# One transformer block on one core: sums of exponentials deferred by the work left, first V products ahead of the rows, last outputs in the scores' PSUM banks

## The chip, the core and the metric

One core of a Trainium2 chip runs the whole program. The metric is the device time of one execution in microseconds (us); the profiler's trace of one such execution gives the times of single instructions. PE is TensorE, DVE is VectorE, ACT is ScalarE, POOL is GpSimd, SP is SyncE, which issues most DMAs here.

## What is computed

Eight sequences (B=8) of N=1024 rows, D=512; context of 1024 rows with 384 columns. Everything is float32. Cut to what matters:

```python
def block(x, ctx, ...):                      # x (8,1024,512)
    # kind 1: cross attention, 8 heads of 64
    y = layernorm(x); q = y @ Wq; k, v = ctx @ Wk, ctx @ Wv
    a = softmax(q k^T / 8); x = x + tanh(g1) * ((a v) @ Wo + bo)
    # kind 2: self attention, 16 heads of 32, with gates over heads
    y = layernorm(x); q, k, v = y @ Wq2 + bq, y @ Wk2 + bk, y @ Wv2 + bv
    q = (q / |q| + query_embedding) * softplus(temperature)
    h = softmax(q k^T / sqrt(32)) v
    gate = top-3 softmax gates of h @ Wr, with the shared gates of h @ Ws   # one number a row
    return x + tanh(g2) * ((h * gate) @ Wp + bp)
```

## The kernel before, in words

**Tiles and stages.** Work on attention goes by chunks of 128 columns of q and k: four chunks of kind 1 (two heads each) and four of kind 2 (four heads each) in each of the eight sequences; below, `one[c]` and `two[c]` are the chunks of a sequence, and a batch is a sequence. A chunk handles the queries in two halves h of 512. A step (`score`, L436, and `value`, L528) takes 128 x 2 x 512 scores twice into two PSUM tiles "sc", ACT makes exponentials "e" of them (two tiles of 128x1024), and PE multiplies e with V into "av". Kind 1 has 8 steps a chunk, kind 2 has 16 (8 in each half).

**Row maxima.** Scores are shifted by their maxima, which have to be known before the chunk's first step. So while one chunk attends, the maxima of the next are taken: PE makes a bf16 copy of the scores ("pm", L373) and DVE reduces it (L414 in pairs of 128x512, L397 in fours). A chunk of kind 2 has 34 such items, kind 1 has 18 (`pairs`, L433; the last two are a small reduction and a transposition). The result goes through four small DMAs into a row "sh" that PE adds to the scores.

**Sums of exponentials.** The softmax needs the sum of e over keys. POOL adds two e tiles (`paired`, L463 to L465); each such pair tile then goes either into an accumulator by an addition on DVE (L473) or stays as a further accumulator (`add`, L469). At the end of a half, `summed` (L483) sums all accumulators over the partitions on PE with a matrix of ones (L491): per round of accumulators 8 matmul records in kind 2 and 4 in kind 1. Then ACT takes Ln and Exp(-x), and POOL multiplies the attended half "hT" by it (`divided`, L519, L526). At most five pair tiles may be live: `room` (L599) empties the queue of postponed work, and where that is not enough sums early into a tile "part".

**What sets the order.** All engines but SP run in an order written out by the program itself. A planner keeps clocks `at["PE"]`, `at["DVE"]`, `at["POOL"]` in ns, with a cost per piece (L220 to L236): 950 for a product of 128 rows (MM), 300 for a pair of maxima on PE and 1380 on DVE, 1750 for an addition on DVE, 1000 for a round of sums. `later` holds postponed work with the clock at which it is due. `attend` (L643) runs a chunk's steps and, between them, fills in products for other stages (`fillers`, up to `cost` ns) and pairs of maxima. It sets `ontime` (L674), which decides in `add` (L472) whether a pair tile may go to DVE:

```python
ontime[0] = not maxima or not maxima.mx or maxima.done >= 1.25 * share * maxima.pairs   # L674
if accs and (self.kind == 1 and self.b or ontime[0] and at["DVE"] <= at["PE"] + 1000):  # L472
```

**The start** (L933 to L959) loads weights, context and rows, makes k of `one[0]`, normalizes and transposes the eight row tiles with five of the eight V products (`v1`, L741) between them, then q; then `pace` (L909) makes the maxima of `one[0]` beside projections. **The end** is `finish` (L782): for each half the gates ("pg"), `weights` (small DVE operations), and `outputs` ("po", L841: product with wp into PSUM, then x = po * gate + x on DVE, L847, and the store, L848). For the last sequence it fills the second half of the last chunk and runs on after it. `ln1` (L709) normalizes and transposes the rows of the next sequence beside `two[2]`; `load_rows` (L695) issues their loads.

Of the kernel before, what the change touches and what calls it, by code (L numbers as in the profile page):

```python
# [10 lines left out]
F32 = mybir.dt.float32  # L11
# [5 lines left out]
P = 128  # L17
# [4 lines left out]
def tile_gated_block(  # L22
# [44 lines left out]
    H = 512  # L67
# [21 lines left out]
        nc.sync.dma_start(out=xt, in_=x[b, ts(t, P), :])  # L89
        return xt  # L90

    def load_ctx(b, parts=1):
        ct = big.tile([P, NDC, N], F32, tag="ctx", name=f"ctx_{b}")
        src = cT[b].rearrange("(c p) n -> p c n", p=P)
        for h in range(parts):
            nc.sync.dma_start(out=ct[:, :, ts(h, N // parts)], in_=src[:, :, ts(h, N // parts)])
        return ct


# [158 lines left out]
    class Chunk:  # L258


        def __init__(self, kind, b, c):
            self.kind, self.b, self.c = kind, b, c
            self.key = f"{kind}_{b}_{c}"
            self.width = HD1 if kind == 1 else HD2
            self.nh = P // self.width
            self.nk = 4 // self.nh
            self.ns = NT // self.nk
            self.mx, self.done, self.free, self.waiting = None, 0, 0.0, False
            self.SC = 2200 if kind == 1 else 1250
            self.steps = [(h, s) for h in range(NH) for s in range(self.ns)]  # L270

# [197 lines left out]
        def add(self, h, s, u, a, last):  # L469

            accs = self.acc.setdefault((h, u), [])
            if accs and (self.kind == 1 and self.b or ontime[0] and at["DVE"] <= at["PE"] + 1000):  # L472
                nc.vector.tensor_tensor(accs[-1], accs[-1], a, ALU.add)  # L473
                dve(1750)
                live[0] -= 1
                ready = at["DVE"] + 500
            else:
                accs.append(a)
                ready = at["PE"]
            if last and s + 1 == self.ns:  # L480
                later.append((ready, self.summed, h, True))

        def summed(self, h, end):  # L483

            ps = gen(f"sum_{self.key}_{h}")
            accs = [self.acc.pop((h, u)) for u in range(self.nh // 2)]
            for n in range(max(map(len, accs))):
                for u, acc in enumerate(accs):
                    for j in range(2):
                        if n < len(acc):  # L490
                            nc.tensor.matmul(  # L491
                                ps[ts(2 * u + j, self.width), :],
                                lhsT=ones[:, 0 : self.width],
                                rhs=acc[n][:, j, :],
                                start=(n == 0),
                                stop=(n == len(acc) - 1),
                            )
# [12 lines left out]
            r = work.tile([P, H], F32, tag="r", name=f"r_{self.key}_{h}", bufs=1)  # L510
            if part is not None:
                nc.vector.tensor_tensor(r, ps, part, ALU.add)
                dve(700)
                ps = r
            nc.scalar.activation(r, ps, AF.Ln)
            nc.scalar.activation(r, r, AF.Exp, scale=-1.0)  # L516
            self.divided(h, r)

        def divided(self, h, r=None):  # L519

            if h not in self.halves:
                self.halves[h] = r
                return
            self.finished.add(h)
            hT, r = self.st.hT[h][:, self.c, :], self.halves[h] if r is None else r
            nc.gpsimd.tensor_tensor(hT, hT, r, ALU.mult)  # L526

        def value(self, step):  # L528

# [5 lines left out]
            for kk in range(self.nk):  # L535
# [13 lines left out]
                    self.paired(h, s, 0, e[0], e[1], True)  # L549
                if kk + 1 < self.nk:  # L550
                    yield
            if self.kind == 2 and s % 2 == 0:
                room(2, self, h)
                for u in range(2):
                    self.paired(h, s + 1, u, e[u], self.e[h, s + 1][u], u == 1)
# [8 lines left out]
        def attention(self, after, first):  # L564

            if first:  # L570
                self.begun()
                yield "begun"
            for m, step in enumerate(self.steps):
                if m + 1 < len(self.steps):
                    self.score(self.steps[m + 1])
                    yield
                elif after:
                    yield "ready"
                    after.begun()
                    yield  # L580
                yield from self.value(step)

        def begun(self):
            self.e, self.acc, self.parts, self.halves, self.finished = {}, {}, {}, {}, set()
            self.score(self.steps[0])

# [1 line left out]
    later, soon = [], []  # L588
    live, ontime = [0], [True]

    def due(ns):
        while soon and soon[0][0] <= ns:
            _, emit, *args = soon.pop(0)
            emit(*args)
        while later and later[0][0] <= ns:
            _, emit, *args = later.pop(0)
            emit(*args)

    def room(n, ch, h):  # L599

        while live[0] > 5 - n:
            if later:
                _, emit, *args = later.pop(0)
                emit(*args)
            else:
                ch.summed(h, False)
        live[0] += n
# [35 lines left out]
    def attend(  # L643
# [20 lines left out]
        def pairs(slack):  # L664
# [2 lines left out]
                return pair(maxima, slack)  # L667
            return bool(ahead and ahead.done + 3 < ahead.pairs and pair(ahead, slack))

        was = at["PE"]  # L670
        for got in ch.attention(after, first):
            attended += at["PE"] - was
            share = max(0, attended / total - since) / (1 - since)
            ontime[0] = not maxima or not maxima.mx or maxima.done >= 1.25 * share * maxima.pairs  # L674
            due(at["PE"])
            if got == "begun":
                fill()
# [28 lines left out]
        rs = small.tile([P, NT, 1], F32, tag="rs1", name=f"rs1_{st.b}")  # L706
        inverse(rs, st.mv)

    def ln1(st):  # L709

        st.yT = big.tile([P, ND, N], F32, tag="yT", name=f"y1T_{st.b}")
        xts = [load_rows(st, t, "xn") for t in range(2)]
        scaled(xts[0], xts[0], st.mv[:, 0, :])
        for t in range(NT):
            if t + 1 < NT:
# [7 lines left out]

    def begin(b):
        st = State()
        st.b = b
# [55 lines left out]
    def finish(st, other=None):  # L782
# [21 lines left out]
        def weights(h):  # L804
# [33 lines left out]
            dve(2600)  # L838
            yield

        def outputs(h):  # L841
            rt = rts[h]
            for t in range(NQ):
                ps = gen(f"po2_{b}_{h}_{t}")
                yield from out_project(ps, hT, w, h * NQ + t)
                x1 = st.x[h * NQ + t]
                nc.vector.scalar_tensor_tensor(x1, ps, rt[:, t, :], x1, ALU.mult, ALU.add)  # L847
                nc.sync.dma_start(out=out[b, ts(h * NQ + t, P), :], in_=x1)  # L848
                dve(750)
                yield  # L850

        if other:
            yield from beside(other, gates(0), ND)
            yield from weights(0)
            yield from beside(outputs(0), gates(1), ND)
            yield from weights(1)
            yield from outputs(1)
            return
        for h in range(NH):
            yield from gates(h)  # L860
            yield from weights(h)
            yield from outputs(h)

    def between(st, nxt):

# [92 lines left out]
    pace(one[0], fill, one[1], (14 + 15 + 14) * MM)  # L958
    run(fill, 1e9)  # L959
    prev = None  # L960
    for b in range(B):
# [20 lines left out]
        fill = [v1(nxt)] if nxt else []  # L982
        attend(two[0], two[1], True, fill, 25 * MM, two[1], two[2])
        two[3].loads()
        attend(two[1], two[2], False, [two[3].project(st)], 19 * MM, two[2], two[3], rate=1.6)
        st.w = load_w(wp2, f"wp2_{b}")
        if nxt:
            one = nxt.chunks[1]
            one[0].loads()
            fill = [ln1(nxt), one[0].project(nxt)]  # L990
            attend(two[2], two[3], False, fill, 9 * 2100 + 16 * MM, two[3], one[0], least=2100)
            one[1].loads()
            attend(two[3], one[0], False, [one[1].project(nxt)], 15 * MM, one[0], one[1])
            prev, st = st, nxt
# [41 lines left out]
```

## Time and profile before

| what | value |
|---|---|
| time, median of 3 runs (lowest, highest) | 5030.72 us (5029.25, 5033.06) |
| the profiled execution's own time | 5029.73 us |
| its span, first to last instruction | 5028.0 us |
| PE busy | 4823.4 us, 96% |
| DVE, POOL, ACT busy | 2908.8, 2552.2, 2314.1 us |
| granted TensorE clock, mean | 0.996 |
| one sequence in the middle (start of `two[0]` to the next) | 621 us |
| first part, until the scores of `one[0]` | 93.4 us |
| last part, after the last product with V | 29.6 us |

How to read it: a group of the profile gives line, engine, operation, tiles and count, then busy time in us and the mean of one in ns, then the idle time of the engine just before them and what ended it. Busy is the union over time, so matmuls that lie side by side in the array count once. In a timeline, a row has start (us), duration (us), engine, line and count, and in brackets the idle time before it with what ended it. Windows by stage have the stretch, its length, and per engine the busy us with the count of instructions.

### The profile page before, as it was taken

To read this page: it belongs to the slowest core of one execution; us is meant where nothing else is said; L and a number is where in the kernel's file an instruction comes from. 1 tells how busy PE (TensorE), PEld (TensorE's weight loads), DVE (VectorE), ACT (ScalarE), POOL (GpSimd) and SP (SyncE) were. 2 spreads that over 40 slices of the span, in tenths; PEclk is the share of its full clock that TensorE was granted. 3 is DMA by queue.
4 is the path that set the end of the run, shared out by engine and by line. 5 is a ranking of instruction groups with operands and counts; after the bars stand their busy time and mean duration, and the time that the engine had idled before them with its cause. 6 is when DMAs were issued, how large, how long until landed. Compare 5 with 4: busy or idle time off the path is not lost.

```text
span 5028.0 us, 83971 instructions
## 1 busy us (share of the span) xinstructions
PE 4823.4 (96%) x35760; PEld 1435.5 (29%) x35760; DVE 2908.8 (58%) x4073; ACT 2314.1 (46%) x3037; POOL 2552.2 (51%) x1352
## 2 busy tenths in 40 slices
PE   8999999999999999999999999999999999999998
PEld 2222232222322223222232222322223322233222
DVE  4556555565555755557555575555755556554665
ACT  3435634356343563435534356343662436524354
POOL 1635646356463664636536365363653636636465
PEclk9999999999999999999999999999999999999999
DMA  2010011100101001010010100101001010010000
GB/s 79 26 32 15 24 42 35 33 17 23 49 26 36 13 23 49 26 36 13 23 52 23 36 13 23 64 11 36 15 23 64 9 36 20 11 51 9 18 1 18
DMA packets 126215, 145.18 MB, mean 29 GB/s; under 512 B 14480, under 2 KB 75920, under 8 KB 125840
## 3 DMA queue, kind: packets, MB, share of 16 engines
q1 hardware_dynamic: 125552, 139.81, 8.7%
q8 instruction: 280, 4.59, 0.4%
q14 instruction: 95, 0.78, 0.0%
q10 hardware_dynamic: 288, 0.00, 0.0%
HBM read 122.47 MB, written 16.78 MB: 28 GB/s over the span
## 4 chain that ended last, share of the span: by engine, by line
PE 81%; DVE 8%; ACT 7%; issue 2%; POOL 1%; DMA 0%; SPq 0%; ACTq 0%; POOLq 0%; DVEq 0%
PE sc L453 21%; PE av L539 17%; PE po L244 8%; PE pq L244 8%; PE pm L373 7%; PE pk L244 7%; PE pv L244 5%; ACT e L460 5%; DVE mx L397 4%; PE sum L491 4%; DVE mx L414 3%; PE pt L215 1%; PE pn L244 1%; POOL e L465 1%; DVE e L473 1%
## 5 line engine op out<-in xcount | busy, mean ns | idle before, releaser
L465 POOL TENSOR_TENSOR e<-e,e 128x1024 f32<-128x1024 f32 x768 | 1850.0, 2424 | 1246.8 <-PE av L539 746.1
L460 ACT ACTIVATE e<-sc 128x1024 f32<-128x1024 f32 x1536 | 1490.1, 1021 | 1275.1 <-PE sc L453 1209.0
L414 DVE TENSOR_REDUCE mx<-pm 128x1 f32<-128x512 f32 x2320 | 1488.7, 686 | 947.6 <-PE pm L373 933.1
L453 PE MATMUL sc<-q,k 32*128 32x512 f32 (+1 forms) x6144 | 1113.4, 606 | 0.0
L539 PE MATMUL av<-e,v 128*32 128x512 f32 (+1 forms) x6144 | 1076.0, 609 | 0.0
L473 DVE TENSOR_TENSOR e<-e,e 128x1024 f32<-128x1024 f32 x402 | 676.2, 1694 | 327.0 <-POOL e L465 326.2
L373 PE MATMUL pm<-kb,qb 32*128 32x512 bf16 (+1 forms) x3072 | 623.1, 382 | 46.2 <-DVE mx L397 26.4
L397 DVE TENSOR_REDUCE mx<-pm 128x2 f32<-128x1024 f32 x376 | 434.8, 1219 | 294.4 <-PE pm L373 294.4
L453 PE MATMUL sc<-sh,ones_b 1*128 1x512 bf16 x3072 | 413.3, 384 | 76.6 <-ACT e L460 67.7
L453 PEld LDWEIGHTS sc<-q,k 32*128 32x128 f32 (+1 forms) x6144 | 419.7, 186 | 191.3 <-issue 184.6
L373 PEld LDWEIGHTS <-qb 32*128 32x128 bf16 (+1 forms) x3072 | 147.6, 91 | 928.0 <-issue 918.4
L539 PEld LDWEIGHTS av<-e,v 128*32 128x32 f32 (+1 forms) x6144 | 193.2, 117 | 602.1 <-issue 571.2
L244 PE MATMUL pq<-y1T,wq 128*32 128x512 f32 (+1 forms) x1568 | 246.9, 595 | 5.3 <-ACT q L308 2.8
L244 PE MATMUL pk<-y2T,wk 128*32 128x512 f32 x2048 | 241.6, 594 | 7.5 <-ACT qq L315 7.5
L244 PE MATMUL pq<-y2T,wq 128*32 128x512 f32 x2048 | 244.9, 595 | 3.2 <-ACT rn L340 3.2
L244 PE MATMUL pv<-wv,y2T 128*32 128x512 f32 x2048 | 241.3, 597 | 0.0
L453 PEld LDWEIGHTS <-ones_b 1*128 1x128 bf16 x3072 | 103.3, 91 | 468.0 <-issue 453.2
L244 PE MATMUL po<-wp,h2T 128*64 128x512 f32 (+1 forms) x1152 | 232.3, 597 | 0.0
L244 PE MATMUL po<-wo,h1T 128*32 128x512 f32 x2048 | 229.9, 594 | 1.1 <-ACT y2T L216 0.9
L491 PE MATMUL sum<-e,ones 128*32 128x512 f32 (+1 forms) x1464 | 224.6, 595 | 3.6 <-DVE e L473 3.4
L526 POOL TENSOR_TENSOR h2T<-h2T,r 128x512 f32<-128x512 f32 x64 | 81.5, 1273 | 250.6 <-ACT r L516 212.8
L244 PE MATMUL pk<-ctx,wk 128*32 128x512 f32 (+1 forms) x1176 | 191.6, 604 | 17.7 <-DMA ctx<-in_ctx 9.0
(108 smaller groups left out, 2885.5 us busy)
## 6 DMA issues: line engine op xcount, KB each, us to landing
x<-in_x SPq DMA_DIRECT2D x64, 256.0 KB
out<-x SPq DMA_DIRECT2D x64, 256.0 KB
xs<-in_x SPq DMA_DIRECT2D x56, 256.0 KB
xn<-in_x SPq DMA_DIRECT2D x56, 256.0 KB
ctx<-in_ctx SPq DMA_DIRECT2D x7, 1536.0 KB
wq<-in_L_xattn_Wq SPq DMA_DIRECT2D x32, 256.0 KB
wo<-in_L_xattn_Wo SPq DMA_DIRECT2D x8, 1024.0 KB
wk<-in_L_ffn_Wk SPq DMA_DIRECT2D x32, 256.0 KB
```

Of the source, the lines that this page charges most:

```text
L215: nc.tensor.transpose(pt[:, c, :], xn[:, ts(c, P)], ident)
L244: nc.tensor.matmul(ps[ts(j, w), :], lhsT=lhsT[:, ts(j, w)], rhs=rhs, start=start, stop=stop)
L373: nc.tensor.matmul(ps, lhsT=self.qb[ts(i, width), ts(c, P)], rhs=self.kb[ts(i, width), ts(kh, H)], start=True, stop=True,)
L397: nc.vector.tensor_reduce(out, tiles[u], AX.X, ALU.max)
L414: nc.vector.tensor_reduce(mx[:, i * NT + c, kh : kh + 1], ps, AX.X, ALU.max)
L453: nc.tensor.matmul(pss[j // 2][:, j % 2, :], lhsT=lhsT, rhs=rhs, start=(m == 0), stop=(m == 1))
L460: nc.scalar.activation(e[u], pss[u], AF.Exp)
L465: nc.gpsimd.tensor_tensor(one, one, two, ALU.add)
L473: nc.vector.tensor_tensor(accs[-1], accs[-1], a, ALU.add)
L491: nc.tensor.matmul(ps[ts(2 * u + j, self.width), :], lhsT=ones[:, 0 : self.width], rhs=acc[n][:, j, :], start=(n == 0), stop=(n == len(acc ...
L526: nc.gpsimd.tensor_tensor(hT, hT, r, ALU.mult)
L539: nc.tensor.matmul(self.av[ts(i, width), :], lhsT=st.v[:, kc, ts(self.c * self.nh + i, width)], rhs=e[j // 2][:, j % 2, :], start=(kc == 0 ...
```

## The change

- `add`: an addition that is not wanted, or for which DVE is over 1000 ns behind and which is not the last of its step, goes back to the head of `later`, due 300 ns on. It is decided for good when it is wanted or when `room` (or the end of a stage) forces it; forced and not wanted, it stays an accumulator as before.
- `ontime` comes from `in_time`: pairs of maxima left against twice the steps left, and their cost against the planned time left less 10000 ns. It also looks at maxima that have not begun (`waiting`).
- The last chunk of the last sequence (`ends`): the e tiles of steps 6 and 7 of each half are not paired on POOL but summed on PE (`whole`); the multiplication by the inverse sum is on DVE; after the last step, `last_outputs(1)` takes the two "sc" tiles, multiplies the heads of chunks 0 to 2 into them, then the gates, then chunk 3.
- The start: context of the first sequence in 6 loads instead of 2, the V weights loaded ahead of all row tiles, a V product in each of the 8 rounds of row tiles, and ahead of the transposition; the filling of `pace` has 28 MM instead of 43.
- `ln1` of the next sequence: its first two loads are issued before `two[1]` attends, its first two scalings are emitted before `two[2]` attends, and its cost is 8 instead of 9 units of 2100. In the last sequence, `two[1]` fills at rate 3 instead of 1.6.

The diff, cut to its core:

```diff
-        for h in range(parts):
-            nc.sync.dma_start(out=ct[:, :, ts(h, N // parts)], in_=src[:, :, ts(h, N // parts)])
+        if b:
+            nc.sync.dma_start(out=ct, in_=src)
+        for h in range(0 if b else NH):
+            for c in range(NDC):
+                nc.sync.dma_start(out=ct[:, c, ts(h, H)], in_=src[:, c, ts(h, H)])
...
+            self.ends = (kind, b, c) == (2, B - 1, ND - 1)
...
-            if accs and (self.kind == 1 and self.b or ontime[0] and at["DVE"] <= at["PE"] + 1000):
+            wanted = self.kind == 1 and self.b or ontime[0]
+            free = at["DVE"] <= at["PE"] + 1000
+            if accs and not forced[0] and not (wanted if free else wanted and last):
+                later.insert(0, (at["PE"] + 300, self.add, h, s, u, a, last))
+                return
+            elif accs and wanted:
...
+            if end:
+                accs = [acc + self.whole.pop((h, u), []) for u, acc in enumerate(accs)]
...
-            nc.gpsimd.tensor_tensor(hT, hT, r, ALU.mult)
+            engine = nc.vector if self.ends else nc.gpsimd
+            engine.tensor_tensor(hT, hT, r, ALU.mult)
...
-            if self.kind == 2 and s % 2 == 0:
+            if self.kind == 2 and s + 2 == self.ns and self.ends:
+                for u in range(2):
+                    self.whole[h, u] = [e[u], self.e[h, s + 1][u]]
+                live[0] += 4
+                later.append((at["PE"] + 3000, self.summed, h, True))
+            elif self.kind == 2 and s % 2 == 0:
...
+        def in_time(share):
+            if not maxima or not (maxima.mx or maxima.waiting):
+                return True
+            pairs = maxima.pairs - maxima.done
+            work = pairs * 1450 + 1750 + max(0, at["DVE"] - at["PE"])
+            steps = (1 - share) * len(ch.steps)
+            return pairs <= 2 * steps - 3 and work <= (1 - share) * (1.1 * total + cost) - 10000
...
-            ontime[0] = not maxima or not maxima.mx or maxima.done >= 1.25 * share * maxima.pairs
+            ontime[0] = in_time(attended / total)
...
+        def last_outputs(h):
+            tiles = [ps_sc.tile([P, 2, H], F32, tag="sc", name=f"po2_{b}_{h}_{u}") for u in range(2)]
...
+            for k in range(ND - 1):
+                for t in range(NQ):
+                    heads(k, t)
+                if k == 1:
+                    due(1e12)
+            for _ in gates(h):
+                pass
+            for t in range(NQ):
+                heads(ND - 1, t)
+            for _ in weights(h):
+                pass
+            for t in range(NQ):
+                scaled_output(h, t, tiles[t // 2][:, t % 2, :])
+        if not other:
+            yield from gates(0)
+            yield from weights(0)
+            yield from outputs(0)
+            yield from iter(lambda: st.through, True)
+            last_outputs(1)
+            return
...
-    st.ct = load_ctx(0, NH)
-    st.x = [load_x(0, t) for t in range(NQ)]
+    st.ct = load_ctx(0)
     st.w = load_w(wv1, "wv1_0")
+    st.x = [load_x(0, t) for t in range(NT)]
     one[0].loads("q")
-    st.x += [load_x(0, t) for t in range(NQ, NT)]
...
+        run(values, NDC * MM)
         if t:
             transposed(was, st.yT, t - 1, "1_0")
-        if t > 2:
-            run(values, NDC * MM)
...
-    fill = [one[1].project(st)] + values + [one[2].project(st)]
+    fill = values + [one[1].project(st), one[2].project(st)]
     constants()
-    pace(one[0], fill, one[1], (14 + 15 + 14) * MM)
+    pace(one[0], fill, one[1], (14 + 14) * MM)
...
-        attend(two[1], two[2], False, [two[3].project(st)], 19 * MM, two[2], two[3], rate=1.6)
+        rows = [load_rows(nxt, t, "xn") for t in range(2)] if nxt else []
+        attend(two[1], two[2], False, [two[3].project(st)], 19 * MM, two[2], two[3], rate=1.6 if nxt else 3)
...
-            fill = [ln1(nxt), one[0].project(nxt)]
-            attend(two[2], two[3], False, fill, 9 * 2100 + 16 * MM, two[3], one[0], least=2100)
+            fill = [ln1(nxt, rows), one[0].project(nxt)]
+            next(fill[0])
+            attend(two[2], two[3], False, fill, 8 * 2100 + 16 * MM, two[3], one[0], least=2100)
```

More of the change, by code (lines that the diff above doesn't have):

```diff
@@ L90, in load_x, with load_ctx @@
         return xt
-    def load_ctx(b, parts=1):
+    def load_ctx(b):
         ct = big.tile([P, NDC, N], F32, tag="ctx", name=f"ctx_{b}")
         src = cT[b].rearrange("(c p) n -> p c n", p=P)
-        for h in range(parts):
-            nc.sync.dma_start(out=ct[:, :, ts(h, N // parts)], in_=src[:, :, ts(h, N // parts)])
+        if b:
[3 more added lines that the diff above has]
+                nc.sync.dma_start(out=ct[:, c, ts(h, H)], in_=src[:, c, ts(h, H)])
         return ct
@@ L581, in attention @@
                 yield from self.value(step)
+            self.st.through = self.ends
         def begun(self):
+            self.whole = {}
             self.e, self.acc, self.parts, self.halves, self.finished = {}, {}, {}, {}, set()
@@ L589, in tile_gated_block, with now @@
     live, ontime = [0], [True]
+    forced = [False]
+    def now():
+        forced[0] = True
+        _, emit, *args = later.pop(0)
+        emit(*args)
+        forced[0] = False
     def due(ns):
@@ L595, in due @@
         while later and later[0][0] <= ns:
-            _, emit, *args = later.pop(0)
-            emit(*args)
+            if ns > 1e11:
+                now()
+            else:
+                _, emit, *args = later.pop(0)
+                emit(*args)
     def room(n, ch, h):
@@ L602, in room @@
             if later:
-                _, emit, *args = later.pop(0)
-                emit(*args)
+                now()
             else:
@@ L707, in stats1, with ln1 @@
         inverse(rs, st.mv)
-    def ln1(st):
+    def ln1(st, xts):
         st.yT = big.tile([P, ND, N], F32, tag="yT", name=f"y1T_{st.b}")
-        xts = [load_rows(st, t, "xn") for t in range(2)]
         scaled(xts[0], xts[0], st.mv[:, 0, :])
@@ L725, in begin @@
         st = State()
-        st.b = b
+        st.b, st.through = b, False
         st.chunks = {kind: [Chunk(kind, b, c) for c in range(ND)] for kind in (1, 2)}
@@ L839, in weights, with scaled_output @@
             yield
+        def scaled_output(h, t, ps):
+            x1 = st.x[h * NQ + t]
+            nc.vector.scalar_tensor_tensor(x1, ps, rts[h][:, t, :], x1, ALU.mult, ALU.add)
+            nc.sync.dma_start(out=out[b, ts(h * NQ + t, P), :], in_=x1)
+            dve(750)
         def outputs(h):
-            rt = rts[h]
             for t in range(NQ):
@@ L845, in outputs, with heads @@
                 yield from out_project(ps, hT, w, h * NQ + t)
[L846 to L849, printed above, removed]
+                scaled_output(h, t, ps)
                 yield
-        if other:
-            yield from beside(other, gates(0), ND)
+        def last_outputs(h):
+            tiles = [ps_sc.tile([P, 2, H], F32, tag="sc", name=f"po2_{b}_{h}_{u}") for u in range(2)]
+            def heads(k, t):
+                by_columns(
+                    tiles[t // 2][:, t % 2, :],
+                    hT[h][:, k, ts(t, P)],
+                    w[:, k, :],
+                    k == 0,
+                    k == ND - 1,
+                )
+            for k in range(ND - 1):
[13 more added lines that the diff above has]
+            yield from gates(0)
             yield from weights(0)
-            yield from beside(outputs(0), gates(1), ND)
-            yield from weights(1)
-            yield from outputs(1)
+            yield from outputs(0)
+            yield from iter(lambda: st.through, True)
+            last_outputs(1)
             return
[L859 to L862, printed above, removed]
+        yield from beside(other, gates(0), ND)
+        yield from weights(0)
+        yield from beside(outputs(0), gates(1), ND)
+        yield from weights(1)
+        yield from outputs(1)
     def between(st, nxt):
```

## The prediction

> **What bounds the kernel now.** I read the page's busy shares and the shares of the chain that ended last, then the groups by line, then windows by stage of a sequence in the middle, then timelines at the start and the end.
>
> ```profile
> PE 4823.4 (96%) x35760; PEld 1435.5 (29%) x35760; DVE 2908.8 (58%) x4073; ACT 2314.1 (46%) x3037; POOL 2552.2 (51%) x1352
> ...
> PE 81%; DVE 8%; ACT 7%; issue 2%; POOL 1%; DMA 0%; SPq 0%; ACTq 0%; POOLq 0%; DVEq 0%
> ...
> L473 DVE TENSOR_TENSOR e<-e,e 128x1024 f32<-128x1024 f32 x402 | 676.2, 1694 | 327.0 <-POOL e L465 326.2
> ...
> L491 PE MATMUL sum<-e,ones 128*32 128x512 f32 (+1 forms) x1464 | 224.6, 595 | 3.6 <-DVE e L473 3.4
> ```
>
> PE is busy 96% and carries 81% of the chain: time goes where PE work goes. The sums (L491) are 224.6 us of it, and each pair tile that DVE adds (L473, 402 of them) is one that PE need not sum. POOL makes 768 pair tiles; 8 sequences x (8 halves of kind 1 + 16 accumulators of kind 2) = 192 must stay, so 174 more could go to DVE. 21 of those fall in each sequence.
>
> The windows of L491 alone, one line each for `two[0]`, `two[1]`, `two[2]`, `two[3]` of sequence 3 (stretch, its length, busy us and count):
>
> ```profile
> 2127.30:2325.00 197.70, 2.12 (x12) 0.36 (x12) 1.00 0.09 29
> 2325.00:2394.70 69.70, 4.84 (x36) 1.18 (x36) 1.00 0.03 8
> 2394.70:2471.80 77.10, 6.76 (x56) 1.90 (x56) 0.98 0.12 35
> 2471.80:2535.90 64.10, 4.68 (x32) 1.14 (x32) 1.00 0.03 9
> ```
>
> A round of 8 records is 0.85 to 0.97 us. `two[0]` is already at the least; the surplus is in `two[2]` (DVE adds 2 there, busy 39.8 of 77.1 us), then `two[1]` and `two[3]` (7 and 8 adds).
>
> **1. The new rule for sums, per sequence.** The old rule asks for 1.25 x share of the maxima; the new one for (a) pairs left <= 2 x steps left - 3 and (b) 1450 x pairs left + 1750 <= (1 - share) x (1.1 x total + cost) - 10000.
> - `two[1]` (total 36000, cost 18050): 9 pairs are ahead at the start. The planner makes about 1.9 pairs a step without additions, while (b) asks for 57650/16/1450 = 2.5 a step. So the new rule says yes until about 0.4 of the chunk, the old until 0.5; both say no until the maxima end. Rounds 2 + 2 + 1 = 5 before, 5 after: nothing.
> - `two[2]` (cost 32000): 5 to 7 pairs are ahead, (a) wants 6 at once and 2 a step. I take no in the first half of the queries, as before (4 rounds). In the second half the fillers have brought some 28 of 34 pairs by share 0.7, where (a) allows 6 left and (b) 7: yes. And an addition that must wait now waits until the maxima are done, where before it became an accumulator at once. So 4 rounds become 1.
> - `two[3]` (maxima of kind 1, 18 items): (a) asks for 11 done by 0.7, the old rule for 16. The two additions refused before go to DVE: 5 rounds become 3 or 4.
>
> That is 4 to 4.5 rounds less, 4 us of PE. Not all is time. A step without filling is bound by ACT (two exponentials of 1.02 us); the waits on ACT stand in the PE timeline of `two[2]`, columns start, us, line, count, idle before:
>
> ```profile
> 2460.30 1.06 PE L539 MATMUL av<-e,v 128*32 128x512 f32 x8
> 2461.18 1.90 PE L491 MATMUL sum<-e,ones 128*32 128x512 f32 x16
> ...
> 2466.36 0.39 PE L453 MATMUL sc<-sh,ones_b 1*128 1x512 bf16 x2 [0.53 <-ACT e L460]
> ...
> 2469.53 0.39 PE L453 MATMUL sc<-sh,ones_b 1*128 1x512 bf16 x2 [0.52 <-ACT e L460]
> ```
>
> From 2460.30 the step with the two rounds lasts 3.90 us, the next ones 3.17: taking 1.73 us of sums from it gives 0.73. So of 4 us I count 2.7.
>
> Added: 8 additions a sequence on DVE. Those of `two[2]` lie where DVE has nothing else (its maxima are through at 2456.3 of 2471.8), the others cost maxima a later start. Free of POOL one takes 1.23 us (the median), the longest 3.38, the mean 1.69: 14 us of DVE, hidden. Where the cover is gone, `two[3]` starts late. Bounds of this part: 4 us gained in full at one end, nothing gained at the other; 9 us if the rule says yes in the first half of `two[2]` and in `two[1]` too.
>
> **2. `ln1` earlier.** PE waits 1.69 us at 2397.6 for the first scaled row tile (ACT L200), which stands behind the exponentials. Emitted before the chunk it goes ahead of them; but the exponentials then end 1.5 us later and the second score step waits for their bank. Between 0 and 1.69 I take 0.7, the transposition (0.66) that comes forward. The two loads (0.37 us of issue each) come one chunk earlier on SP, which has then nothing waiting.
>
> Parts 1 and 2: 3.4 us x 7 sequences = **24 us**.
>
> **3. The start.**
>
> ```profile
> 8.98 7.31 PE L244 MATMUL pk<-ctx,wk 128*32 128x512 f32 x48 [8.98 <-DMA ctx<-in_ctx]
> 19.04 0.63 PE L215 MATMUL pt<-ident,xn 128*128 128x128 f32 x4 [2.76 <-ACT xn L200]
> 20.53 1.12 PE L215 MATMUL pt<-ident,xn 128*128 128x128 f32 x4 [0.86 <-ACT xn L200]
> ```
>
> The loads run at about 400 KB a us from 6 us on, so the first of six pieces lands near 6.7 instead of 8.98: 2.3 us. The V weights land by about 12.5, before the k products end at 14.0, so the waits of 2.76, 0.86 and 0.83 go, and with them the V product at half clock (4.29 against 2.78 us). All eight V products are done at 40.4; before it was five at 41.5. So `pace` has 8.3 us less to do. But its maxima end as late as before less 1.1 us (80.2, now 79), since the small constants on DVE (49.4 to 56.1) still stand ahead of them, and from there to the landed row is 5 to 6 us (nm, transposition, rows, four DMAs of 0.7 us, landing 1.7). With the filling used up, PE idles some 4.5 us. Scores begin at 85 instead of 93.4: 8 us. Given back: the 8 pairs of `one[1]` that had been taken ahead (8 x 0.32 = 2.6 us), and, as 18 pairs are then left against 2 x 8 - 3, no addition in the first half of `one[0]`: 3 more accumulators of 1.08 us. Left: **2 us**, between -4 and 8.
>
> **4. The last sequence.** In `two[2]` maxima end after the steps, and PE stands in the chain row by row:
>
> ```profile
> 4928.59 0.39 PE L423 MATMUL pr<-ident,nm 128*32 128x128 f32 x1 [1.68 <-DVE nm L419]
> 4931.02 2.62 PE L453 MATMUL sc<-sh,ones_b 1*128 1x512 bf16 x4 [2.04 <-DMA sh<-rows]
> 4933.07 2.28 PE L453 MATMUL sc<-q,k 32*128 32x512 f32 x8
> ```
>
> About 5 us of idle, then 3 us at half clock (2.28 us for records that take 1.24 later). Rate 3 brings the projection, and with it pairs, earlier, and refused additions leave DVE to the maxima. Between 0 and 8 plus two rounds of sums I take **5 us**.
>
> **5. The end.**
>
> ```profile
> 5001.77 1.07 PE L491 MATMUL sum<-e,ones 128*32 128x512 f32 x8 [3.39 <-DVE e L473]
> 5010.26 13.95 PE L244 MATMUL po<-wp,h2T 128*32 128x512 f32 x127
> ```
>
> The stall of 3.39 us goes, with two POOL and two DVE additions ahead of it. Added: two rounds in each half (4 x 0.9). The 13.95 us of outputs are split: 10.4 ahead of the gates, 3.5 beside the gate's small operations (2.9 us). What is late next is DVE: four outputs of 0.75 now end one after another, 3.0 instead of 0.75, then the store (2.95) as before. The multiplication on DVE stands by L512 (0.69) against 1.27 on POOL. The first half is through about two steps earlier, so fewer of its outputs are left over (48 records, 5.2 us). With them the idle time of the steps from 4965.9 to 4976.2 is used (0.5 to 0.8 a step, 2.54 ahead of the gates: 2.5 in all), and the exponentials that waited for DVE (0.23 and 0.86) go. Sum: -3.4 + 3.6 + 2.25 - 2.5 - 1.1 = about **-1 us**, between -6 and 4.
>
> **Sum.** 24 + 2 + 5 + 1 = 32 us, from the profiled execution's 5029.7 (span 5028.0 and 1.7 around it): 4998; the median of the runs shown lies 1 us above it: **4999 us**.
>
> **Rivals.**
> - *More goes to DVE* (0.15). If pairs run ahead of (a) early in `two[2]`, all 21 surplus accumulators go: 9 us of part 1 instead of 2.7, 7 times, 44 us more: 4955. For: DVE is idle for half of `two[2]`. Against: 5 pairs ahead where 6.1 are asked.
> - *The rule refuses as often as the old one* (0.17). The reserve of 10000 ns is a sixth of the planned time of `two[1]`, about the old rule's fifth. If no round goes, the pairs of part 4 are not gained either, and 0.7 x 7 + 2 + 1 = 8 us are left: 5023.
> - *DVE becomes the bound* (0.14), slower. Additions behind a POOL addition last up to 3.38 us, planned at 1.75: 1.6 x 8 = 13 us late a sequence. It decides once the maxima of `two[3]` or of the next `one[0]` end after the steps; the price is the 8 us of part 4, here 7 times: 56 - 32 = 24 us slower, 5055. For: 103 additions waited 326 us on POOL. Against: DVE is busy 39.8 of 77.1 and 38.5 of 64.1 us. The Trainium skill, in "SBUF — State Buffer", section "SBUF: two separate sides", states that a DVE operation with two SBUF inputs and a GpSimd operation that reads SBUF exclude each other for a whole instruction. The trace agrees as far as it goes (1.23 us free, up to 3.38); by that rule every added addition that meets POOL is late.
>
> **Chances.** Forecast 0.54 (its own range 4980 to 5015), rivals as above. A measurement of this kernel tells 0.2% (10 us) from no change: faster (below 5020.7) 0.54 + 0.15 + 0.01 = 0.70; same 0.16; slower 0.14. Range 4962 to 5034: it leaves out half of the first rival and most of the last.
>
> **What would show it.** L491: 7 x 4 x 8 = 224 records fewer, of which about 60 come back in the first and the last sequence; L473 near 450; L504 (early sums) falls from 26 to about 18. The wait of 1.69 at the first transposition gone; first PE record near 6.7; `two[2]` 2.5 us shorter; no 3.39 at the last sum. Wrong: L491 unchanged, `two[2]` or `two[3]` longer, or PE waiting on "sh" in a sequence other than the last.

## The result, and the profile after

The changed kernel takes 5005.09 us (median of 6 runs, 5003.89 to 5007.73) against 5030.22 for the kernel before (6 runs): a ratio of 0.995, 95% interval 0.9938 to 0.9963, so 25 us less where 32 were forecast. The profiled execution took 5004.68 us, its span is 5002.9, the mean granted clock 0.996 as before. The total came out near the forecast by luck: the terms were off in both directions, and their errors cancelled, as the experiments show.

The lines of the changed kernel's page that answer to those shown of before (DVE's additions are now L483, the sums L503):

```profile
PE 4803.4 (96%) x35660; PEld 1427.7 (29%) x35660; DVE 2988.2 (60%) x4111; ACT 2309.3 (46%) x3036; POOL 2567.5 (51%) x1346
...
PE 78%; DVE 9%; ACT 7%; issue 4%; POOL 2%; DMA 1%; SPq 0%; ACTq 0%; DVEq 0%; POOLq 0%
...
L483 DVE TENSOR_TENSOR e<-e,e 128x1024 f32<-128x1024 f32 x431 | 760.1, 1779 | 347.2 <-POOL e L470 345.4
...
L503 PE MATMUL sum<-e,ones 128*32 128x512 f32 (+1 forms) x1364 | 204.2, 596 | 0.0
```

PE is busy 20.0 us less, and the sums are 20.4 us less: it looks as if the sums had paid for the change. But DVE has gone from 8 to 9% of the chain that ended last, and its additions have grown from a mean of 1694 ns to 1779.

The windows of the sums (L503) alone, one line each for `two[0]` to `two[3]` of sequence 3 (stretch, length, busy us and count):

```profile
2117.40:2315.10 197.70, 2.12 (x12) 0.36 (x12) 1.00 0.09 29
2315.10:2383.50 68.40, 4.01 (x32) 0.84 (x32) 1.00 0.03 8
2383.50:2456.30 72.80, 4.86 (x40) 1.20 (x40) 1.00 0.13 36
2456.30:2520.90 64.60, 4.01 (x32) 0.94 (x32) 1.00 0.03 8
```

`two[2]` has lost 16 records and 4.3 us, `two[1]` 4 records and 1.3 us; `two[3]` has kept 32 and is 0.5 us longer (2.2 us in two of the seven sequences, where the clock is halved for 3.4 us). Where the changed kernel stands at the ends of parts, against before: 3.1 us behind when `one[3]` of the first sequence ends, 25.9 ahead when `two[3]` of the seventh does, 20.4 ahead at the last product with V, 25.1 ahead at the end of the span.

Start and end, as forecast: the first record at 6.60 instead of 8.98, the V products behind it without a wait, and no 3.39 us ahead of the last sum; of the last outputs 12.2 us stand ahead of the gates and 3.65 behind.

```profile
6.60 8.02 PE L247 MATMUL pk<-ctx,wk 128*32 128x512 f32 x48 [6.60 <-DMA ctx<-in_ctx]
14.43 5.34 PE L247 MATMUL pv<-wv,ctx 128*32 128x512 f32 x48
19.70 0.66 PE L218 MATMUL pt<-ident,xn 128*128 128x128 f32 x4
...
4977.78 2.76 PE L503 MATMUL sum<-e,ones 128*32 128x512 f32 x24
4980.35 12.20 PE L247 MATMUL po<-wp,h2T 128*32 128x512 f32 x112
...
4993.51 3.65 PE L247 MATMUL po<-wp,h2T 128*32 128x512 f32 x31
```

Three places in the changed kernel where PE stands, from its timeline (start, us, line, count, idle before): the first scores, `one[0]` of the first sequence, and `two[3]` of sequence 3.

```profile
83.22 0.39 PE L458 MATMUL sc<-sh,ones_b 1*128 1x512 bf16 x1 [2.49 <-DMA sh<-rows]
84.58 1.26 PE L458 MATMUL sc<-sh,ones_b 1*128 1x512 bf16 x3 [0.98 <-DMA sh<-rows]
85.77 3.79 PE L458 MATMUL sc<-q,k 64*128 64x512 f32 x8
...
132.08 0.58 PE L378 MATMUL pm<-kb,qb 64*128 64x512 bf16 x1 [2.59 <-DVE mx L419]
...
133.13 3.79 PE L458 MATMUL sc<-q,k 64*128 64x512 f32 x8
...
2480.92 0.37 PE L378 MATMUL pm<-kb,qb 64*128 64x512 bf16 x1 [1.77 <-DVE mx L419]
```

The last two waits are new. PE stands before a pair of maxima ("pm"), because DVE is still at an addition and hasn't reduced the pair before it, so no PSUM bank is free. DVE and POOL around the wait in `two[3]`:

```profile
2473.61 6.66 DVE L483 TENSOR_TENSOR e<-e,e 128x1024 f32<-128x1024 f32 x2
2480.19 2.47 DVE L419 TENSOR_REDUCE mx<-pm 128x1 f32<-128x512 f32 x4
2482.58 2.35 DVE L483 TENSOR_TENSOR e<-e,e 128x1024 f32<-128x1024 f32 x2
```

```profile
2473.53 2.36 POOL L470 TENSOR_TENSOR e<-e,e 128x1024 f32<-128x1024 f32 x1
2476.70 5.79 POOL L470 TENSOR_TENSOR e<-e,e 128x1024 f32<-128x1024 f32 x2 [0.81 <-ACT e L465]
```

Two additions take 6.66 us beside POOL's, the next two 2.35 us once POOL is through.

### The profile page after: what moved, and what is told of

Its sections match the earlier page's. It is cut to its first block, busy times and chain, and to the rows that moved or that the text cites. A ratio compares the mean times of both kernels' runs of the same rounds, so it can differ in the third digit from the quotient of the medians.

```text
span 5002.9 us, 83870 instructions
## 1 busy us (share of the span) xinstructions
PE 4803.4 (96%) x35660; PEld 1427.7 (29%) x35660; DVE 2988.2 (60%) x4111; ACT 2309.3 (46%) x3036; POOL 2567.5 (51%) x1346
## 4 chain that ended last, share of the span: by engine, by line
PE 78%; DVE 9%; ACT 7%; issue 4%; POOL 2%; DMA 1%; SPq 0%; ACTq 0%; DVEq 0%; POOLq 0%
PE sc L458 21%; PE av L552 16%; PE po L247 8%; PE pq L247 8%; PE pm L378 7%; PE pk L247 6%; PE pv L247 6%; ACT e L465 5%; DVE mx L402 4%; PE sum L503 3%; DVE mx L419 3%; POOL e L470 2%; PE pt L218 1%; DVE e L483 1%; PE pn L247 1%
## 5 line engine op out<-in xcount | busy, mean ns | idle before, releaser
L419 DVE TENSOR_REDUCE mx<-pm 128x1 f32<-128x512 f32 x2336 | 1496.3, 685 | 981.6 <-PE pm L378 969.2
L483 DVE TENSOR_TENSOR e<-e,e 128x1024 f32<-128x1024 f32 x431 | 760.1, 1779 | 347.2 <-POOL e L470 345.4
L378 PE MATMUL pm<-kb,qb 32*128 32x512 bf16 (+1 forms) x3072 | 625.5, 383 | 60.4 <-DVE mx L402 25.9
L503 PE MATMUL sum<-e,ones 128*32 128x512 f32 (+1 forms) x1364 | 204.2, 596 | 0.0
L347 POOL TENSOR_TENSOR qq<-qq,rn 128x512 f32<-128x512 f32 x64 | 88.3, 1379 | 220.0 <-ACT rn L346 220.0
```

What stands on the lines that cost most here:

```text
L347: nc.gpsimd.tensor_tensor(self.qq, self.qq, rn, ALU.mult)
L378: nc.tensor.matmul(ps, lhsT=self.qb[ts(i, width), ts(c, P)], rhs=self.kb[ts(i, width), ts(kh, H)], start=True, stop=True,)
L419: nc.vector.tensor_reduce(mx[:, i * NT + c, kh : kh + 1], ps, AX.X, ALU.max)
L503: nc.tensor.matmul(ps[ts(2 * u + j, self.width), :], lhsT=ones[:, 0 : self.width], rhs=acc[n][:, j, :], start=(n == 0), stop=(n == len(acc ...
```

## The experiments

Twelve further kernels ran. Times are medians of 4 to 11 runs; the kernel before, run again beside them, was at 5029 to 5030, and the changed kernel is taken at the 5005.1 above. A ratio is against the kernel before, with its 95% interval.

**1. The rule alone.** To the kernel before, the hunks of `add`, `in_time`, `now`, `due` and `room` are added, nothing else.

> The kernel before with the new rule for sums alone: the new in_time and the putting off of an addition, everything else as before. By its written-out order it makes 426 additions on VectorE, where the kernel before makes 402. Theory (the gain of the whole change is TensorE time of sums that VectorE takes over, about 0.9 us for a round of 8 records, in the seven sequences that another follows): 18 to 24 us faster than before, so 5006 to 5012. Rival A (the gain comes from ln1 being earlier and from idle time that goes, the sums hardly matter): 0 to 10 us faster. Rival B (the rule is worth more and the start and the end take some of it back): 30 us faster or more.

Measured: **5057.17**, ratio 1.0054 (1.0041 to 1.0068): 28 us slower. All three theories fall. The rule does what it says (sums from 1464 to 1368 records), and PE is busy 3 us more. From PE's timeline in `two[2]` of sequence 3:

```profile
2404.30 1.90 PE L496 MATMUL sum<-e,ones 128*32 128x512 f32 x16
2409.14 0.66 PE L215 MATMUL pt<-ident,xn 128*128 128x128 f32 x4 [2.94 <-ACT xn L200]
```

The wait for the first row tile, 1.69 before, is now 2.94. `two[2]` takes 79.4 us instead of 77.1, `two[3]` up to 66.4 instead of 64.1.

**2. All but the rule.** The changed kernel with the two old lines back:

```diff
-            wanted = self.kind == 1 and self.b or ontime[0]
-            free = at["DVE"] <= at["PE"] + 1000
-            if accs and not forced[0] and not (wanted if free else wanted and last):
...
+            if accs and (self.kind == 1 and self.b or ontime[0] and at["DVE"] <= at["PE"] + 1000):
...
-            ontime[0] = in_time(attended / total)
+            ontime[0] = not maxima or not maxima.mx or maxima.done >= 1.25 * share * maxima.pairs
```

> The changed kernel with the old rule for sums (1.25 x share, and decided at once), all else as changed. 404 additions by its order, where the changed kernel makes 431. Theory (sums carry the gain): about 20 us slower than the changed kernel, 5022 to 5028. Rival A (ln1, start and end carry it): 5005 to 5012.

Measured: **4994.98**, ratio 0.9932 (0.992 to 0.9945): 10 us faster than the changed kernel, against the theory and outside rival A too. `two[2]` takes 71.0 us with the 56 sum records that it had before. So the gain per sequence is not made of sums.

**3 and 4. The rule's two halves.** Run 3 puts off but asks the old question (`ontime[0]` as above); run 4 asks the new question but decides at once:

```diff
-            if accs and not forced[0] and not (wanted if free else wanted and last):
...
-            elif accs and wanted:
+            if accs and wanted and (free or self.kind == 1 and self.b):
```

> The changed kernel with the old 1.25 x share as its question, but an addition still put off while the answer is no. 441 additions by its order against 431. Theory (the putting off is what saves the rounds, the new bound of pairs and work saves nothing): the same as the changed kernel or up to 4 us faster, 5001 to 5006. Rival (the new bound keeps maxima ahead of the last step; without it VectorE is late somewhere): slower than the changed kernel by 5 us or more, with a wait on nm, pr or sh at the end of a chunk.

Measured: **5031.07**, ratio 1.0005 (0.9995 to 1.0014). The rival holds: 441 additions, the fewest sums so far, and 26 us slower than the changed kernel. Waits on the row "sh" come to 27.1 us (10.6 in the changed kernel), as maxima end behind the steps.

> The changed kernel with the new bound of pairs and work, but decided at once: a refused addition becomes an accumulator of its own, as in the kernel before. 364 additions by its order against 431 (134 x 2 sum records more than the changed kernel). Theory (rounds of sums are TensorE time, and the bound alone refuses more than the old one): 20 to 30 us slower than the changed kernel, 5025 to 5035, so no faster than before. Rival (steps without filling are bound by ScalarE, so the rounds lie beside it): under 12 us slower than the changed kernel.

Measured: **5052.50**, ratio 1.0046 (1.0033 to 1.0058). It is 47 us slower than the changed kernel, beyond the theory's 20 to 30: besides the sums (1632 records) PE now waits up to 3.5 us for DVE in `two[3]`. PE's longest waits in this kernel (who, for whom: us in total, times, longest):

```profile
PE sc L458 <- ACT e L465: 72.4, 168, 3.7
PE pm L378 <- DVE mx L419: 34.0, 50, 3.5
```

and the same view of the changed kernel and of the kernel of run 9 below (old rule, new end):

```profile
PE pm L378 <- DVE mx L419: 21.6, 36, 2.6
```

```profile
PE pm L378 <- DVE mx L419: 5.3, 23, 0.4
```

**5, 6 and 7. `ln1` alone, in two pieces.** Run 5 is the kernel before with the three edits of `ln1`; run 6 keeps the count of 9, run 7 changes the count alone:

```diff
+        rows = [load_rows(nxt, t, "xn") for t in range(2)] if nxt else []      # 5, 6: ahead of two[1]
...
-            fill = [ln1(nxt), one[0].project(nxt)]
-            attend(two[2], two[3], False, fill, 9 * 2100 + 16 * MM, two[3], one[0], least=2100)
+            fill = [ln1(nxt, rows), one[0].project(nxt)]                       # 5, 6
+            next(fill[0])                                                      # 5, 6
+            attend(two[2], two[3], False, fill, 8 * 2100 + 16 * MM, two[3], one[0], least=2100)  # 5, 7
```

> The kernel before with the earlier ln1 alone: its two loads one chunk earlier, its first scaling ahead of the chunk, and 8 instead of 9 fillings counted. By its order 409 additions against 402. Theory L (found in the two runs that part the rule from the rest: the stage two[2] went from 75.5 to 77.1 us to 71.0 with the sums unchanged, so ln1 gives about 5 us in each of 7 sequences, and the rule gives nothing): 4990 to 4997. My prediction's size for this step (0.7 us a sequence): 5025. Rival (ln1 gains only together with the new start or the new rule): 5010 or above.

Measured: **4993.31**, ratio 0.9926 (0.9913 to 0.994): 36 us faster than before, as theory L says, and seven times the size that the prediction gave this step.

> As the run before it in this list, but the plan still counts 9 fillings of 2100 ns. 402 additions, as before the change. Theory L1 (it is the row tiles standing ready ahead of the first transposition that counts: the waits of 1.69, 0.86 and 0.39 us go and the clock stays up): 4990 to 5000. Rival L2 (it is the count: with 8 the filling is spread over more steps, and fewer steps at the end of the chunk are bound by ScalarE): 5015 to 5025.

Measured: **4998.01**, ratio 0.9939 (0.9926 to 0.9951): theory L1, within its range. The edit also issues the two loads earlier, but that can't be the cause: between the issues at 2164.42 and 2400.03 us in the kernel before, and at 2149.93 and 2383.77 in run 5, there is no load of rows, so the first two tiles lay ready long before in both. What moved is their scaling on ACT.

> The kernel before with nothing changed but the count of 8 instead of 9 fillings. 395 additions. Theory L1: 5030 to 5040, no gain, since the waits for the row tiles stay. Rival L2: 5005 or below.

Measured: **5040.83**, ratio 1.0022 (1.0013 to 1.0031): L2 falls; the count alone costs 11 us. It helps (4.7 us) only where the rows stand ready.

How one early instruction gives 5 us a sequence: windows of `two[2]` of sequence 3 in the kernel before, cut into four (stretch, length, PE, PEld, DVE, ACT, POOL busy with counts, granted clock, DMA share, GB/s), then in run 5:

```profile
2394.70:2412.00 17.30, 14.98 (x124) 5.41 (x122) 11.63 (x18) 14.52 (x20) 9.36 (x5) 1.00 0.17 47
2412.00:2430.00 18.00, 16.63 (x127) 6.60 (x126) 10.75 (x17) 11.76 (x17) 9.68 (x5) 0.91 0.25 73
2430.00:2456.30 26.30, 25.04 (x213) 7.43 (x216) 17.42 (x29) 12.84 (x16) 14.06 (x8) 1.00 0.03 9
2456.30:2471.80 15.50, 14.25 (x123) 3.78 (x116) 0.00 (x0) 8.62 (x12) 8.68 (x5) 1.00 0.06 19
```

```profile
2380.10:2397.40 17.30, 16.99 (x140) 6.26 (x136) 12.17 (x18) 16.86 (x24) 10.74 (x6) 1.00 0.24 68
2397.40:2415.40 18.00, 17.33 (x154) 6.03 (x152) 11.36 (x18) 12.17 (x16) 10.44 (x5) 1.00 0.16 54
2415.40:2439.60 24.20, 23.98 (x212) 7.20 (x209) 16.09 (x26) 10.87 (x13) 11.58 (x6) 1.00 0.03 9
2439.60:2451.20 11.60, 10.35 (x89) 2.81 (x82) 0.00 (x0) 7.41 (x11) 8.68 (x5) 1.00 0.09 25
```

In the first 17.3 us PE is busy 2.0 us more and ACT 2.3: the tile that is scaled ahead lets the first two transpositions go out at once, and no later one waits for its own scaling. PE's idle time in the four stretches is 2.32, 1.37, 1.26 and 1.25 us before and 0.31, 0.67, 0.22 and 1.25 in run 5: 3.75 us less in a stage that is 6.0 us shorter. In the second stretch the clock stays at 1.00 instead of 0.91; before, it fell there behind two gaps of 0.39 and 0.86 us at doubled transpositions:

```profile
2416.87 1.37 PE L215 MATMUL pt<-ident,xn 128*128 128x128 f32 x8 [0.39 <-ACT part L504]
2418.17 0.40 PE L373 MATMUL pm<-kb,qb 32*128 32x512 bf16 x2
2419.43 1.09 PE L215 MATMUL pt<-ident,xn 128*128 128x128 f32 x4 [0.86 <-ACT y1T L216]
```

Half clock is the smaller part of the gain, though. The same two gaps stand in all seven sequences of the kernel before, but the clock of these 18 us is 0.91 in three of them, where `two[2]` takes 77.1 us, and 1.00 in the four others, where it takes 75.5 to 75.9. The stretch behind the last maximum is shorter (11.6 us instead of 15.5) as more of the work lies ahead of it; its idle time is 1.25 us in both.

**8 and 9. The end, and the rate.** Run 8 is the changed kernel with the old rule, the old end (the old branch of `finish`, `self.ends = False`) and `rate=1.6` throughout; run 9 keeps the new end.

> The changed kernel with the old rule for sums, the old end and the old rate of 1.6: what is left of the change is ln1 and the start. 406 additions. Theory (ln1 5 us a sequence, the start 3 us, while the rule costs about 10 us and the new end and rate cost some 6 us in the last sequence): 4987 to 4991, the fastest so far. Rival (the new end pays for itself, as predicted): 4996 or above, slower than the changed kernel with the old rule alone (4995).

Measured: **4988.18**, ratio 0.992 (0.9906 to 0.9933): the theory. It differs from run 5 by the start alone: 5 us. In the profiled executions the start takes between 2.8 us less and 0.9 more than before among four kernels that share the new one and the old rule, so "1 to 5 us gained" is all that I would say.

> The changed kernel with the old rule for sums and the old rate of 1.6 in the last two[1], but with the new end in full. Beside the run with old rule and old end (4988.2) it prices the end alone; beside the run with the old rule alone (4995.0) it prices the rate alone. Theory (the new end costs two[3] about 7 us for additions of POOL and VectorE that hold each other and for 16 more sum records, and gives back 5 behind the last product): 4989 to 4992, 1 to 4 us slower than with the old end; the rate accounts for the other 3 to 6 us. My prediction's size (end 1 us gained, rate 5 us gained): 4987 for this one, and it would be 5 us slower than with rate 3.

Measured: **4987.14**, ratio 0.9916 (0.9902 to 0.9929), **the fastest**, 18 us below the changed kernel. The end is worth 1 us, within the scatter, and not the loss that the theory expected: `two[3]` grows from 57.8 to 62.7 us and what follows the last product with V shrinks from 31.4 to 24.1. Against run 2, which differs in the rate alone, it is 8 us faster: the rate of 3 costs 8. By stage of the last sequence, run 2 takes 2.4 us more in `two[1]`, 0.6 less in `two[2]`, 5.5 more in `two[3]` and 0.9 more behind the last product. In `two[1]`, the projection of `two[3]` is placed ahead of maxima that `two[2]` needs, and their row comes late: the transposition "pr" of its maxima starts at 4824.93 in run 2, 2.0 us later than in run 9, and PE stands at the first scores of `two[2]`:

```profile
4828.75 0.41 PE L458 MATMUL sc<-sh,ones_b 1*128 1x512 bf16 x1 [2.22 <-DMA sh<-rows]
4829.43 1.94 PE L458 MATMUL sc<-sh,ones_b 1*128 1x512 bf16 x3 [0.26 <-DMA sh<-rows]
4830.79 2.08 PE L458 MATMUL sc<-q,k 32*128 32x512 f32 x7
```

The larger part, in `two[3]`, comes from the same additions in another order. In run 2 four of them stand one behind the other on DVE (11.07 us) beside four of POOL (11.23), ACT waits 2.36 us for a tile, and PE waits for ACT; in run 9 they come two and two (4.50 and 4.49 us), and PE waits for ACT 0.75 at most. PE in run 2, then the windows of `two[3]` in run 2 and in run 9 (columns as above):

```profile
4920.34 0.39 PE L458 MATMUL sc<-sh,ones_b 1*128 1x512 bf16 x2 [2.11 <-ACT e L465]
...
4900.00:4968.40 68.40, 59.70 (x588) 17.84 (x588) 28.33 (x37) 33.18 (x39) 31.62 (x13) 0.90 0.03 13
4897.00:4961.40 64.40, 57.33 (x600) 17.18 (x596) 26.06 (x37) 34.77 (x40) 30.31 (x13) 0.97 0.04 14
```

Why the rate of `two[1]` brings these additions together two stages later was not followed up.

**10. The split of the last outputs alone.** As run 9, but

```diff
-            if self.kind == 2 and s + 2 == self.ns and self.ends:
+            if False:
...
-            engine = nc.vector if self.ends else nc.gpsimd
+            engine = nc.gpsimd
```

> As the run before it in this list, but of the new end only the last outputs that begin in the scores' banks ahead of the gates: the last two key tiles of a half are paired and added as before, and the last multiplication stays on POOL. The stall of 3.4 us at the last sum is back. Theory (the outputs ahead of the gates give the 4 to 5 us behind the last product, and the rest of the end is what costs): 4984 to 4987, the fastest. Rival (the whole sums are what brings the gates forward, so that the split alone is worth nothing): 4988 to 4992.

Measured: **4991.19**, ratio 0.9924 (0.9912 to 0.9937). The theory falls and the rival holds: without the whole sums the stall at the last sum stays ahead of everything, and the split is worth nothing by itself (3 us slower than run 8).

**11. Additions only where POOL is free by the plan.**

```diff
-            free = at["DVE"] <= at["PE"] + 1000
+            free = at["DVE"] <= at["PE"] + 1000 and at["POOL"] <= at["PE"]
```

> The changed kernel in full, but its rule asks for one thing more before an addition goes to VectorE: that POOL has nothing to do by the plan. 438 additions by its order against 431. Theory C (the rule costs because more of its additions meet a POOL addition and last 2 to 3.4 us instead of 1.2, with maxima and TensorE behind them): fewer than 30 additions of 3 us or more (47 in the changed kernel, 23 before), no wait of 1.77 us on mx in two[3], and 5 to 12 us faster than the changed kernel: 4993 to 5000. Rival D (it costs because it moves pairs and sums to other steps, whatever an addition lasts): within 4 us of the changed kernel, 5001 to 5009.

Measured: **5023.37**, ratio 0.9989 (0.998 to 0.9998), 18 us slower than the changed kernel. The edit did not do what it was made for: additions of 3 us or more went from 47 to 73, as the plan's clock for POOL isn't POOL's. More long additions and a longer time go together here, as theory C would have it, but `two[1]` also lost 2 of its 8 additions and is 3.6 us longer; both theories miss their ranges, and the run does not part C from D. Over all runs the count of long additions does not give the order of the times: run 3 has 30 and run 12 has 27, fewer than the changed kernel, and both are slower.

**12. Every addition of `two[2]` to DVE.** Run 9 with

```diff
+            ontime[0] = ontime[0] or bool(fillers) and ch.kind == 2 and ch.c == 2
```

> The kernel of the run with the old rule and the new end (4987.1), but in two[2] of the seven sequences that another follows every addition goes to VectorE at once as soon as it is planned free, whatever the maxima are at: 9 additions there by its order where that kernel makes none, 36 sum records of two[2] fewer, 4.3 us of TensorE a sequence by 0.95 us for 8 records. Theory S (the steps of two[2] with a transposition are bound by ScalarE, which is busy 16.9 of the first 17.3 us, so a round taken from TensorE there only uncovers a wait): two[2] between 70 and 73 us, busy TensorE 3 to 4 us less and idle time as much more; 4980 to 4995. Prediction's theory (a round that goes is worth 0.73 us where a step isn't filled and up to its whole length where it is): two[2] 67 to 68 us, 4957 to 4966. Third (maxima come late for the last step): two[2] or two[3] with a wait on pr or sh, above 5000.

Measured: **5068.96**, ratio 1.0075 (1.0061 to 1.0088). `two[2]` takes 82.9 us instead of 71.0, so only the third theory is left, which set no upper bound: `two[3]` is 5.8 us shorter, the next `one[0]` 4.6 longer. The last steps of `two[2]` in sequence 3, from PE's timeline:

```profile
2486.52 0.28 PE L428 MATMUL pr<-ident,nm 128*32 128x128 f32 x1
2489.79 2.67 PE L458 MATMUL sc<-sh,ones_b 1*128 1x512 bf16 x4 [2.99 <-DMA sh<-rows]
2491.88 2.28 PE L458 MATMUL sc<-q,k 32*128 32x512 f32 x8
```

Maxima end at 2483.1, then reduction, transposition, DMAs and landing stand in the open, and the clock is 0.71 over the last 23.5 us. Waits on "sh" come to 46.5 us in the whole kernel. So the run shows what late maxima cost; what a round is worth while the maxima stay in time it does not show.

## Why the prediction was right in total and wrong in its parts

The runs make a chain in which one part at a time is added. Differences of medians, in us:

| part | predicted | measured | from, to |
|---|---|---|---|
| `ln1` earlier | -5 (0.7 x 7) | -36 | before, run 5 |
| the start | -2 | -5 | run 5, run 8 |
| the end | -1 | -1 | run 8, run 9 |
| the rate of 3 | (-5, with the rule) | +8 | run 9, run 2 |
| the rule for sums | -19 (2.7 x 7) | +10 | run 2, changed kernel |
| all | -32 | -25 | |

The rule's price depends on what stands beside it: 28 us alone on the kernel before, 10 us at the end of the chain.

- **What bounds the kernel.** That PE carries the chain was read rightly; that a record taken from PE is therefore time was not. PE's busy time holds records at half clock, and its order hides waits that open when a round goes. Against run 2 the changed kernel has PE busy 9.8 us less (4803.4 against 4813.2) and idle 19.3 us more: waits for "mx" (L419) ahead of "pm" grow from 4.8 to 21.6 us, and waits ahead of the transpositions "pt" from 3.1 to 14.1.
- **Step 1, the rule. This failed.** "So 4 rounds become 1" in `two[2]` and "So of 4 us I count 2.7": 16 records went there, 4 in `two[1]`, none in `two[3]`, 100 in all instead of 164 (431 additions where some 450 were forecast). And they were not worth 2.7 us but less than nothing. By stage, changed kernel against run 2: `two[1]` -1.3 us; `two[2]` +1.8; `two[3]` +0.6 to 2.3; the next `one[0]` +0.8, `one[1]` -0.8: 11 us over the seven sequences; the end of the first sequence's `one[0]` is 7.6 late, of which the stages behind it give back 3.4; the last sequence gives back 5.6. In `two[2]` the records go, but idle time rises from 2.4 to 5.0 us: sums that were put off come out ahead of the row tiles, two transpositions then fall into one step, and the second waits 1.07 us for ACT's copy:

```profile
2386.50 1.90 PE L503 MATMUL sum<-e,ones 128*32 128x512 f32 x16
...
2395.64 0.65 PE L218 MATMUL pt<-ident,xn 128*128 128x128 f32 x4 [1.07 <-ACT y1T L219]
```

- **Step 2, `ln1`. Mis-sized by seven.** "Between 0 and 1.69 I take 0.7": the wait for the first tile was taken to be all that could go. What went were the waits of 1.69, 0.86, 0.44 and 0.40 us and some shorter ones in `two[2]`, 3.75 us in all; in three of the seven sequences 3.4 us at half clock went with them, worth 1.6. The later waits and the clock were terms that the prediction had put at nothing.
- **Step 3, the start.** First record at 6.60 (6.7 predicted), V products without a wait from 14.43, scores at 83.22 (85): as predicted, and with the old rule in place the sum of 2 us lies in the "1 to 5" of run 8. In the changed kernel the rule takes it back: the addition at 128.04 lasts 3.39 us where that of run 2 lasts 1.22.
- **Step 4, the last sequence. Wrong sign.** "Rate 3 brings the projection, and with it pairs, earlier": it brings the projection, and takes PE's time from the pairs that are due first. Most of the 8 us lies further on, in `two[3]`, which this step didn't look at. The wait on "sh" at 4931 is still there (2.53 us, up to 4903.55, in the changed kernel).
- **Step 5, the end.** Right in sum (1 us). One term was off: the multiplication on DVE took 2.52 us, not 0.69, as it met a POOL addition (5.10 us for two); the gates waited 2.90 for it.
- **The rivals.** The one that ended slower, DVE as the bound, is right in part. Runs 3 and 4 lie 26 and 47 us above the changed kernel and run 12 82 above run 9, each with PE waiting on "mx" or "sh". In the changed kernel DVE is late too, but not in the way that this rival named: maxima do not end after the steps (from 300 to 4790 us no wait on "sh" is over 0.3 us); PE waits for a bank of maxima instead (the 1.77). `ln1` hid it. That a POOL addition beside it is what makes an addition long is borne out by durations: of 431 additions, the 165 with no POOL instruction beside them take 1.207 to 1.226 us, and the 47 of 3 us or more have 2.86 us of POOL beside them on average (23 such before). But not every addition that meets POOL is late, as the prediction took it to be: 66 of the other 266 take less than 1.3 us. That these 24 more are the rule's whole price is argued, not shown: run 11 was to tell and could not.

## What to carry to other kernels

A total that fits proves no term: run each part alone, and all but that part, before explaining a gain. Work taken off the engine that is busy all the time is worth nothing where it lay in front of a wait; ask what the next instruction waits for once it is gone. Where an in-order engine feeds the busy one, having one tile ready a step ahead can be worth several times the wait at the first tile: smaller waits at the later tiles go with it (here 3.75 us for a first wait of 1.69), and sometimes half clock.

## What was not expected of the hardware

- **The clock can fall after short gaps.** Behind 2.59 us of idle PE in the changed kernel, scores took 3.79 us instead of 1.99, and the granted clock was 0.83 from 120 to 140 us. The length of a gap alone does not decide it: the same gaps of 0.39 and 0.86 us in `two[2]` of the kernel before stood ahead of 0.91 in three sequences and of 1.00 in four, and of the seven waits for maxima in `two[3]` of the changed kernel (1.75 to 2.10 us) two were followed by half clock. What decides it, no run here shows. The Trainium skill, in "TensorE: Matmul & The Clock Gate", section "HAM oscillation — how this bites in real kernels", asks for no gaps over about 3.4 us. Here a shorter one, of 2.59 us, was followed by half clock, so the measurement decides: that figure is no safe distance.
- **A small DVE operation can wait as long as a large one.** The multiplication of 128x512 (L539 in the changed kernel) took 2.52 us beside a POOL addition and 0.69 with none beside it.
